# The shared chunk's product on GpSimd in place, and tables of finer steps of their own for the middle and last attention layers

## The chip, the cores and the metric

The kernel runs on one core of a Trainium2 chip. The metric is the device time of one execution in microseconds (us); the median of three runs is given. The core has TensorE (PE, matmul; its weight loads are PEld), VectorE (DVE), ScalarE (ACT), GpSimd (POOL) and SyncE (SP), each with an instruction queue of its own that runs in order. POOL and SP also issue the transfers (DMAs) of this kernel.

## The reference, cut to what matters

A graph network of four layers over N = 1024 nodes, B = 16 graphs and 128 features, all with the same adjacency matrix `adj`, in which about 8 of 1024 entries of a row are set. Layers L0, L2 and L3 are attention layers with 8 heads of 16 features, and L1 is a graph attention layer with one score per pair.

```python
# L0, L2, L3 (h is the layer's input)
Q, K, V = (h @ Wq, h @ Wk, h @ Wv)                 # heads of 16
scores = where(adj == 0, -inf, Q . K / sqrt(16))   # per head
x = h + (softmax(scores) @ V) @ Wo + bo
x = layer_norm(x, ln1_g, ln1_b)
x = layer_norm(x + relu(x @ W1 + b1) @ W2 + b2, ln2_g, ln2_b)
# L1
g = x @ W
e = leaky_relu(g @ a_src [i] + g @ a_dst [j]); e = where(adj == 0, -inf, e)
x = layer_norm(softmax(e) @ g + x, ln_gamma, ln_beta)
```

## The kernel before, in words

The kernel uses that the matrix is sparse. A setup sorts the nodes and makes lists of edges; the layers then fetch only the rows that edges name.

**Blocks.** The work is cut into 64 blocks, called units in the code: four layers, in each two halves of the graphs (GR = 2, eight graphs each), in each eight groups of 128 rows (T = 8). A row of a block has 8 graphs x 128 features = 1024 numbers (ROW).

**Parts and chunks.** The edges of a block are put into nine chunks. A chunk gives each of the 128 partitions one edge, and it is gathered as one transfer of 128 table rows, keys and values, from DRAM into a buffer `e` (L965, on POOL). Eight of the chunks belong to one group of 32 destination rows each. The ninth, the shared chunk (called MIX), takes the edges that are left over from two or three groups. An attention block has five parts: pairs of chunks are parts 0, 1, 2 and 4, and the shared chunk alone is part 3.

For each part of an attention block, DVE does three things in this order:

- `products`, L977: `pr` = keys of `e` times the queries. The queries of a pair lie in `qr`; those of the shared chunk in `qx`, which `shared` (L943) puts together by two to four SP copies from `qr`. There is one buffer `qx`, and four buffers `pr`.
- `exponentials`, L1000: sums of `pr` over the 16 features of a head; ACT then takes the exponential (`ex`, L1004).
- `weighted`, L1028: `pr` = values of `e` times `ex`, written over the products. It is done one part later.

PE then adds the rows of `pr` into `acc` with matrices of marks (`summed`, L1044), one to two parts later, and the exponentials likewise into the denominators. `divided` takes the reciprocal of the denominators (L1081) and makes `o` from `acc` (L1084), once per block, on DVE; POOL adds two small tiles into `seen` (L1097) for a check at the end.

**Gathers.** There are four buffers `e`, and gathers are issued up to four parts ahead: after the weighting of part i-1, POOL issues the gathers of part i+3 into the buffer that became free. `gathered` is called in this order by the main loop, one call per part.

**Tails.** What follows `o` in a block (output projection, normalisation, the two layers of the network behind it, second normalisation, and the next layer's keys and values) is `attention_tail` and `finish`. It runs in two halves, a and b, as generators of 18 steps each, during the next block. Steps of `attention_tail` are: transposes of `o` (PE, ACT copy), bias (ACT), Wo and `centre` (PE), normalisation in three steps (ACT), transposes, W1 in two steps (PE, ACT), W2 in two steps (PE), normalisation in three steps (ACT), transposes; then, in L0 and L2, two steps of the next layer's keys and values (`project`, PE and ACT, with SP stores to `kept`, L575, and `table`, L592 or L617), or, in L3, the transposes back into `outs` and the store of the output by POOL (L699).

**What sets the order.** Every engine runs its instructions in the order in which the program writes them; nothing is reordered. The main loop writes, for each part, the DVE work above, and between it calls `others()` three times. After an attention block, each of these 15 calls is an opening with a number, and a table gives the steps written there: `PLANS[layer][opening]` is a string in which `a` and `b` are one step of that half's tail and `q` is one step aside (the queries of the next block: Wq on PE, an ACT copy, four repeating matmuls on PE, four ACT copies into `qr`; then loads). Opening 0 comes at the end of part 1 of a block, right after the reciprocal and `o`; 1 to 3 lie in part 2, 4 to 6 in part 3, 7 to 9 in part 4, 10 to 12 in part 0 of the next block, and 13 and 14 in its part 1. Layer 1 has no table and spreads its steps evenly.

In part 1 the copies into `qx` are written after opening 13 and before opening 14, so on SP they stand ahead of every store of opening 14 and behind every store written before.

Of the kernel before, what the change touches and what calls it, by code (L numbers as in the profile page):

```python
# [18 lines left out]
ALU = mybir.AluOpType  # L19
# [29 lines left out]
ROW = G * D  # L49
# [17 lines left out]
MIX = J  # L67
# [51 lines left out]
def of_piece(v, piece):  # L119

    a, b = piece[0][0], piece[-1][0]
    if len(piece) == 2 and a == b:
        return v[:, a : a + 1].to_broadcast([v.shape[0], 2, v.shape[2]])
    return v[:, a : b + 1 : max(b - a, 1)]
# [21 lines left out]
def sparse_path(ctx: ExitStack, tc: tile.TileContext, a: dict, out: bass.AP, flag):  # L146


    nc = tc.nc
# [667 lines left out]
    def at_once(g):  # L817
# [12 lines left out]
        for t in range(T):  # L830
# [12 lines left out]

    PLANS = {
        0: (
            "qaaqqba", "baqba", "aq", "a", "bbaa", "abq", "baqbbaa", "", "aqbbba", "", "bbqaa", "b", "", "qqqqbbqq", "ba",
        ),
        2: (
            "qaaqqba", "baqba", "aq", "a", "bbaa", "abq", "baqbbaa", "", "aqbbba", "", "bbqaa", "b", "", "qqqqbbqq", "ba",
        ),  # L850
        3: (
            "qaaqqba", "baqba", "aq", "a", "bbaa", "abq", "baqbbaa", "", "aqbbba", "", "bbqaa", "b", "", "qqqqbbqq", "ba",
        ),
    }
    plan = [()]
# [6 lines left out]
    parts = []  # L862
# [7 lines left out]
    es, prs, exs, qs, qx, ofs, accums = {}, {}, {}, {}, {}, {}, {}  # L870

    def is_attention(u):
        return LAYERS[units[u][0]][1] is ATTN
# [76 lines left out]
    def gathered(i):  # L950
        if i >= len(parts):
            return
        u, pieces = parts[i]
        if u == T:
            while slow:
                while busy[0] and not held[0]:
                    advance(tails)
                advance(slow)
        l, g, t = units[u]
        width = tables[l, g].shape[1]  # L960
        many = 2 if is_attention(u) else J
        e = gather_buffer()
        es[i] = e[:, : many * width].rearrange("p (k c) -> p k c", k=many)
        for k, (j, r) in enumerate(sum(pieces, [])):
            nc.gpsimd.indirect_dma_start(  # L965
                out=es[i][:, k, :], out_offset=None, in_=tables[l, g][:, :],
                in_offset=bass.IndirectOffsetOnAxis(
                    ap=idx[:, min(l, 1), t, COLUMN[t, j, r] : COLUMN[t, j, r] + 1], axis=0
                ),
                bounds_check=N - 1, oob_is_err=False,  # L970
            )

    def products(i):
        u, (piece,) = parts[i]
        n = len(piece)
        prs[i] = [prods.tile([P, 2, ROW], F32, tag="pr", name="pr")]
        nc.vector.tensor_tensor(  # L977
            prs[i][0][:, :n, :], es[i][:, :n, :ROW],
            qx[u].rearrange("p (o c) -> p o c", o=1) if (MIX, 0) in piece
            else of_piece(qs[u], piece),  # L980
            ALU.mult,
        )

    def exs_of(i):

# [185 lines left out]
    with tc.manual_schedule():  # L1171
        wide = [gather_buffer() for _ in range(EDGES)]
        setup, entry, weights = graph(wide), at_once(0), load_weights("L0")
        next(setup)
        next(weights)
        next(entry)
        more = [weights, load_graph_weights()]
        rest = slots()
        first, second = loaded(0), loaded(1)
        for i, room in enumerate(setup):  # L1180
            if i == T:
                for gen in more:
                    next(gen)
            if room == "load":
                next(first)
            elif room == "spread":
                for _ in entry:
                    pass
                next(rest)
            elif room == "slots":  # L1190
                next(rest)
                for _ in first:
                    pass
                for _ in queries(0):
                    pass
                slow.append(at_leisure(1))
            elif room == "gather":
                for k in range(AHEAD - 1):
                    gathered(k)
                next(second)  # L1200
            else:
                for _ in range(room):
                    if next(entry, "end") == "end":
                        advance(slow)
                        break
        scratch.close()
        prods = ctx.enter_context(tc.tile_pool(name="prods", bufs=4))
        smalls = ctx.enter_context(tc.tile_pool(name="smalls", bufs=3))
        nc.gpsimd.memset(wide[3], 0.0)
        gathered(AHEAD - 1)  # L1210
        fronts.extend([islice(rest, WAIT + 2), second] + more)
        closing, sizes = None, ()
        begun = 0
        for i in range(len(parts) + 2):
            here = i < len(parts)
            u = parts[i][0] if here else len(units)
            if here:
                l = units[u][0]
                eager[0] = 1 if u < 2 else 0
                if i and parts[i - 1][0] != u:  # L1220
                    begun = i
                    if u < T - 1:
                        fronts.append(islice(rest, WAIT + 2))
                    if l + 1 < len(LAYERS) and LAYERS[l + 1][1] is ATTN:
                        if units[u][1:] == (0, 1):
                            more = load_weights(LAYERS[l + 1][0])
                            next(more)
                            next(more)
                        if units[u][1:] == (0, 4):
                            fronts.append(more)  # L1230
                if is_attention(u):
                    products(i)
            if i > 1:
                summed(i - 2)
                done = parts[i - 2][0]
                if parts[i - 1 : i] == [] or parts[i - 1][0] != done:
                    closing = divided(done)
                    next(closing)
            others()
            if here:  # L1240
                exponentials(i)
            if here and i == begun + 1:
                if is_attention(u):
                    shared(u)
                while loads:
                    advance(loads)
                if u + 1 < len(units):
                    fronts.append(queries(u + 1))
                loads.append(loaded(u + 2))
                if u:  # L1250
                    advance(loads)
            others()
            if 0 < i <= len(parts):
                weighted(i - 1, 0)
                if not is_attention(parts[i - 1][0]):
                    others()
                    weighted(i - 1, 2)
                gathered(i - 1 + AHEAD)
                for _ in sizes:
                    pass  # L1260
            if closing is not None and here:
                while any(gen not in free for gen in tails):
                    if opening[0] is None:
                        advance(tails)
                    else:
                        planned("ab")
                while opening[0] is not None and opening[0] < len(plan[0]):
                    planned()
                next(closing)
                sizes, closing = closing, None  # L1270
                passes = 3 if is_attention(u) else 4
                steps = STEPS if is_attention(done) else GRAPH_STEPS
                steps -= LATE[units[done][0]]
                pace[:] = 0.0, steps / (passes * sum(part[0] == u for part in parts) - 1)
                if is_attention(done) and opening[0] is None:
                    for gen in list(tails):
                        if gen in free:
                            for _ in gen:
                                pass
                            tails.remove(gen)  # L1280
                opening[0] = 0 if is_attention(done) else None
                plan[0] = PLANS.get(units[done][0], ())
            others()
            if i + 1 >= len(parts) or parts[i + 1][0] != u:

                while fronts:
                    advance(fronts)
        while opening[0] < len(plan[0]):
            planned()
        while tails:  # L1290
            advance(tails)
        for _ in closing:
            pass
        while tails:
            advance(tails)
# [435 lines left out]
```

## Time and profile before

| what | value |
|---|---|
| median of three runs | 2157.91 us (2153.96 to 2158.05) |
| the profiled execution's own time | 2143.22 us |
| its span, first to last instruction | 2141.5 us |
| mean granted TensorE clock | 0.97 |
| busy: PE, DVE, ACT, POOL | 91%, 86%, 71%, 49% of the span |
| mean DMA rate | 297 GB/s |
| DVE, shared chunk's products | 48 x 1.218 us |
| DVE, products of a pair | 192 x 2.30 us |
| POOL, gathers | 576 x 1.57 us, 8.1 us from issue to landing (median) |

Durations and waits come from the one profiled execution, which was about 15 us shorter than the median of the three runs. L0 takes the first third of the span (to about 707 us), L1 from there to about 1026 us, L2 to about 1580 us, and L3 the rest. Busy times of PE are modelled, since matmuls are pipelined. A wait row reads: who waited, for whom, how many us in all, how often, the longest.

### The profile page before, as it was taken

What the parts mean: (1) busy time and instruction counts of PE and PEld (TensorE: products, weight loads), DVE (VectorE), ACT (ScalarE), POOL (GpSimd) and SP (SyncE); (2) the same over time, 40 slices, a digit from 0 to 9 for tenths busy, and PEclk for the clock granted to TensorE, in tenths of its full rate; (3) what the DMA queues carried; (4) which work ended last, traced back from release to release, by engine and by line L of the source; (5) the groups of instructions that cost most, each with busy time, mean ns of one, the idle gap of its engine ahead of it and who ended that gap; (6) DMA issues with size and microseconds to landing.
All of it is one profiled execution on the core that took longest, in us unless ns stands there. A gap on an engine that the chain in (4) does not pass through costs nothing.

```text
span 2141.5 us, 37070 instructions
## 1 busy us (share of the span) xinstructions
PE 1954.5 (91%) x13444; PEld 1237.4 (58%) x13444; DVE 1852.2 (86%) x1368; ACT 1522.8 (71%) x5043; POOL 1048.6 (49%) x699
## 2 busy tenths in 40 slices
PE   6769999999999988997999999999998999898986
PEld 5545666666655555554566565666655555555554
DVE  6977999999997666677899999999998998989993
ACT  3437878878886554555687887778886878776874
POOL 3333445555456576784354544444443545545540
PEclk8789999999999999999999999999999999999998
DMA  7978888988988799998898998989988878687860
GB/s 272 348 271 291 309 300 313 312 287 316 318 314 288 271 324 323 347 376 309 295 338 310 334 312 293 321 324 319 320 303 297 288 277 297 233 311 260 313 227 22
DMA packets 164800, 636.10 MB, mean 297 GB/s; under 512 B 34664, under 2 KB 37480, under 8 KB 116110
## 3 DMA queue, kind: packets, MB, share of 16 engines
q0 software_dynamic: 88720, 485.08, 63.5%
q1 hardware_dynamic: 75888, 148.57, 20.5%
q8 instruction: 108, 1.77, 0.3%
q14 instruction: 84, 0.69, 0.1%
HBM read 581.08 MB, written 92.34 MB: 314 GB/s over the span
## 4 chain that ended last, share of the span: by engine, by line
PE 68%; DVE 11%; ACT 8%; issue 6%; DMA 4%; POOL 2%; POOLq 0%; DVEq 0%; ACTq 0%
PE acc L1044 17%; PE yps L752 7%; PE ps L654 7%; PE ps L738 7%; PE ps L583 6%; PE ps L929 6%; PE yps L728 4%; PE yps L727 4%; DMA e<-table,idx 4%; PE yps L756 3%; DVE pr L1028 3%; PE ps L920 2%; DVE pr L977 2%; DVE sc L1000 2%; ACT qr L932 2%
## 5 line engine op out<-in xcount | busy, mean ns | idle before, releaser
L965 POOL DMA_INDIRECT e<-table,idx x576 | 903.6, 1569 | 899.0 <-DVE pr L1028 708.8
L1028 DVE TENSOR_TENSOR pr<-e,ex 128x2048 f32<-128x2048 f32 (+1 forms) x320 | 662.2, 2077 | 56.8 <-ACT ex L1016 29.6
L1044 PE MATMUL acc<-pr,marks 128*32 128x512 f32 x2656 | 516.1, 605 | 36.3 <-DVE pr L1028 18.3
L977 DVE TENSOR_TENSOR pr<-e,qr 128x2048 f32<-128x2048 f32 x192 | 441.8, 2301 | 83.2 <-PE acc L1044 30.4
L1000 DVE TENSOR_REDUCE sc<-pr 128x128 f32<-128x2048 f32 (+1 forms) x240 | 497.4, 2073 | 8.1
L631 ACT ACTIVATE z<-yps,root 128x128 f32<-128x128 f32 x888 | 312.9, 368 | 70.4 <-PE yps L756 55.6
L1044 PEld LDWEIGHTS acc<-pr,marks 128*32 128x32 f32 x2656 | 109.7, 110 | 297.6 <-issue 246.9
L752 PE MATMUL yps<-W,f 128*128 128x128 f32 x1520 | 253.6, 285 | 16.9 <-ACT f L747 16.9
L752 PEld LDWEIGHTS yps<-W,f 128*128 128x128 f32 x1520 | 203.4, 191 | 99.3 <-ACT f L747 60.2
L647 ACT ACTIVATE z<-yps,rstd 128x128 f32<-128x128 f32 x888 | 251.0, 367 | 1.6
L587 ACT COPY kv<-ps 128x512 f32<-128x512 f32 x176 | 102.8, 588 | 175.3 <-PE ps L583 160.0
L932 ACT COPY qr<-ps 128x512 f32<-128x512 f32 x384 | 202.9, 602 | 22.2 <-PE ps L929 19.9
L583 PE MATMUL ps<-Wkv,xT 128*128 128x256 f32 x768 | 204.1, 409 | 12.7 <-ACT xT L660 5.5
L747 ACT ACTIVATE f<-ps,b 128x512 f32<-128x512 f32 x190 | 130.4, 687 | 87.9 <-PE ps L738 87.8
L738 PE MATMUL ps<-x,W 128*128 128x512 f32 x384 | 187.0, 610 | 1.3 <-ACT x L662 1.3
L631 ACT ACTIVATION_READ_ACCUMULATOR z<-yps,root 128x1 f32 x888 | 184.4, 208 | 0.0
L583 PEld LDWEIGHTS ps<-Wkv,xT 128*128 128x128 f32 x768 | 145.1, 201 | 67.5 <-issue 14.0
L654 PE MATMUL ps<-ident,z 128*128 128x128 f32 x896 | 148.9, 283 | 37.1 <-ACT qr L932 27.5
L654 PEld LDWEIGHTS ps<-ident,z 128*128 128x128 f32 x896 | 106.1, 142 | 89.0 <-ACT qr L932 62.3
L929 PE MATMUL ps<-q,rep 32*128 32x512 f32 x768 | 146.7, 663 | 8.6 <-ACT q L924 7.6
L727 PE MATMUL yps<-Wo,oT 128*128 128x128 f32 x768 | 153.2, 282 | 0.2
L728 PE MATMUL yps<-centre,x 128*128 128x128 f32 x768 | 152.6, 281 | 0.5 <-ACT x L723 0.2
(174 smaller groups left out, 2526.1 us busy)
## 6 DMA issues: line engine op xcount, KB each, us to landing
table<-kv SPq DMA_DIRECT2D x88, 512.0 KB, 7.5
kept<-xT SPq DMA_DIRECT2D x96, 256.0 KB, 5.1
x<-kept SPq DMA_DIRECT2D x48, 512.0 KB, 7.9
qx<-qr SPq DMA_DIRECT2D x54, 256.0 KB, 6.7
e<-table,idx POOLq DMA_INDIRECT x576, 8.1
table<-kv SPq DMA_DIRECT2D x32, 256.0 KB, 8.1
qx<-qr SPq DMA_DIRECT2D x48, 128.0 KB, 5.0
qx<-qr SPq DMA_DIRECT2D x12, 384.0 KB, 4.6
```

The costliest lines, as they stand in the source:

```text
L583: nc.tensor.matmul(ps[:, k, :], x[:, i + k, :], w[LAYERS[l][0], "Wkv"], start=True, stop=True,)
L631: nc.scalar.activation(z[:, i, :], y[:, i, :], AF.Square, scale=D**-0.5, bias=root, accum_out=total[:, i : i + 1],)
L647: nc.scalar.activation(z[:, i, :], y[:, i, :], AF.Copy, scale=rstd[:, i : i + 1])
L654: nc.tensor.transpose(ps[:, i, :], z[:, i, :], ident)
L738: nc.tensor.matmul(ps, p["W1"][:, f * P : (f + 1) * P], x1.rearrange("p g n -> p (g n)"), start=True, stop=True,)
L752: nc.tensor.matmul(ps[:, i, :], f1[:, f, i * P : (i + 1) * P], p["W2"][:, f, :], start=(f == 0), stop=False,)
L929: nc.tensor.matmul(ps, rep_of(j), q[32 * j : 32 * j + 32], start=True, stop=True)
L965: nc.gpsimd.indirect_dma_start(out=es[i][:, k, :], out_offset=None, in_=tables[l, g][:, :], in_offset=bass.IndirectOffsetOnAxis(ap=idx[:, ...
L977: nc.vector.tensor_tensor(prs[i][0][:, :n, :], es[i][:, :n, :ROW], qx[u].rearrange("p (o c) -> p o c", o=1) if (MIX, 0) in piece else of_p ...
L1000: nc.vector.tensor_reduce(sc[:, :n, :], prs[i][0][:, :n, :].rearrange("p k (a d) -> p k a d", d=HD), mybir.AxisListType.X, ALU.add,)
L1028: nc.vector.tensor_tensor(prs[i][k0 // 2][:, :m, :].rearrange("p k (a d) -> p k a d", d=d), es[i][:, k0 : k0 + m, base : base + ROW].rearr ...
L1044: nc.tensor.matmul(outs[32 * j : 32 * j + 32], marks[:, mark, :], rhss, start=(chunk == mine[0]), stop=(chunk == mine[-1]),)
```

## The change

Two parts. First, the product of the shared chunk is no longer made by DVE into a `pr` buffer but by GpSimd, over the queries in `qx` itself. It is written two parts ahead, behind the gathers of the part that is being written: for part 3 of a block that is at the end of part 1, behind the gathers of part 4. Its sum, its weighting (also in place, on DVE) and PE's sums then read `qx`, so `qx` stays in use until PE has summed the shared chunk. Second, L2 and L3 get tables of their own; the table of L0 stays as it was.

```diff
     PLANS = {
         0: (
-            "qaaqqba", "baqba", "aq", "a", "bbaa", "abq", "baqbbaa", "", "aqbbba", "", "bbqaa", "b", "", "qqqqbbqq", "ba",
+            "qaaqqba", "baqba", "aq", "a", "bbaa", "abq", "baqbbaa", "",
+            "aqbbba", "", "bbqaa", "b", "", "qqqqbbqq", "ba",
         ),
         2: (
-            "qaaqqba", "baqba", "aq", "a", "bbaa", "abq", "baqbbaa", "", "aqbbba", "", "bbqaa", "b", "", "qqqqbbqq", "ba",
+            "aabbqaaqaba", "", "qqa", "bb", "q", "", "b", "aaqba",
+            "", "aqaqbqqba", "qaqbqbbqb", "qb", "a", "", "baaabbb",
         ),
         3: (
-            "qaaqqba", "baqba", "aq", "a", "bbaa", "abq", "baqbbaa", "", "aqbbba", "", "bbqaa", "b", "", "qqqqbbqq", "ba",
+            "q", "qaabqaba", "", "qa", "aq", "qb", "ba", "qbbaqa",
+            "b", "aaqabb", "qb", "bqa", "ababb", "qqbq", "qaaabbb",
         ),
     }
...
     def products(i):
         u, (piece,) = parts[i]
+        if i in prs:
+            return
         n = len(piece)
         prs[i] = [prods.tile([P, 2, ROW], F32, tag="pr", name="pr")]
         nc.vector.tensor_tensor(
             prs[i][0][:, :n, :], es[i][:, :n, :ROW],
-            qx[u].rearrange("p (o c) -> p o c", o=1) if (MIX, 0) in piece
-            else of_piece(qs[u], piece),
+            of_piece(qs[u], piece),
             ALU.mult,
         )
+
+    def product_of_shared(i):
+
+        if i >= len(parts):
+            return
+        u, pieces = parts[i]
+        if not is_attention(u) or (MIX, 0) not in pieces[0]:
+            return
+        own = qx[u].rearrange("p (o c) -> p o c", o=1)
+        prs[i] = [own]
+        nc.gpsimd.tensor_tensor(own, es[i][:, :1, :ROW], own, ALU.mult)
...
                 gathered(i - 1 + AHEAD)
+                product_of_shared(i + 2)
                 for _ in sizes:
                     pass
```

## The prediction

> **What bounds the kernel now.** I read the busy rows of the page first, then stretches by layer, then the chain of waits by layer, then the waits of each engine, and last the order in time of one block. A block is one of the 64 units (layer, half of the graphs, 128 rows); its mark T0 is its reciprocal L1081.
>
> ```profile
> PE 1954.5 (91%) x13444; PEld 1237.4 (58%) x13444; DVE 1852.2 (86%) x1368; ACT 1522.8 (71%) x5043; POOL 1048.6 (49%) x699
> ```
> Three resources are nearly full. By stretches (PE, PEld, DVE, ACT, POOL busy; clock; DMA share; GB/s), steady parts of L0, L2, L3:
> ```profile
> 234.80:647.30 412.50, 395.80 (x2909) 256.00 (x2910) 392.31 (x237) 340.95 (x1180) 207.64 (x130) 1.00 0.88 308
> 1064.50:1580.30 515.80, 494.35 (x3345) 317.08 (x3346) 485.66 (x279) 414.31 (x1320) 240.37 (x149) 1.00 0.90 319
> 1616.40:2071.30 454.90, 417.50 (x2790) 255.12 (x2789) 421.11 (x235) 345.65 (x1120) 229.07 (x144) 0.97 0.80 283
> ```
> They hold 12, 15 and 13 blocks: 34.4, 34.4 and 35.0 us each. PE is 96%, 96% and 92% busy, DVE 95%, 94% and 93%. L3 projects no keys and values and still is no shorter: it waits.
>
> The chain of waits of 1064 to 1580 (L2) is PE with 3.2% on ACT qr L932, 2.0% on ACT f L747 and 1.7% on ACT kv L587, 6.9% or 2.4 us per block, and no DVE line among its thirteen. That of 1616 to 2037 (L3) has 11.5% on the landing of e and 14% on three DVE lines. So L2 hangs on PE's order, L3 on DVE and gathers too. One block of L2 (start, us, engine, line, tiles, idle before):
> ```profile
> 1512.84 0.55 DVE L1081 RECIPROCAL both<-ps 128x64 f32<-128x64 f32 x1
> 1513.42 1.29 DVE L1084 TENSOR_TENSOR o<-acc,both 128x512 f32<-128x512 f32 x2
> 1514.62 2.28 DVE L977 TENSOR_TENSOR pr<-e,qr 128x2048 f32<-128x2048 f32 x1
> 1516.94 2.29 DVE L1000 TENSOR_REDUCE sc<-pr 128x128 f32<-128x2048 f32 x1
> 1519.14 2.28 DVE L1028 TENSOR_TENSOR pr<-e,ex 128x2048 f32<-128x2048 f32 x1
> 1521.34 1.22 DVE L977 TENSOR_TENSOR pr<-e,qx 128x1024 f32<-128x1024 f32 x1
> 1522.59 1.22 DVE L1000 TENSOR_REDUCE sc<-pr 128x64 f32<-128x1024 f32 x1
> ...
> 1532.88 2.29 DVE L977 TENSOR_TENSOR pr<-e,qr 128x2048 f32<-128x2048 f32 x1 [0.85 <-DMA e<-table,idx]
> ```
> See the removed product at 1521.34 (T0+8.5), and 11.5 us later the next block's first product waiting for its gather. That gather is issued after the weighting of 1519.14 frees its buffer. So the removed instruction lies inside the gather's flight: removing it lets DVE arrive earlier at a wait.
>
> **What the Trainium skill says.** "SBUF — State Buffer", Who interferes with whom: a VectorE instruction with two SBUF inputs and a GpSimd instruction that reads SBUF block each other whole; the first holds the port, and tensor_reduce never contends. The trace agrees: the small GpSimd sum
> ```profile
> 1524.74 1.62 POOL L1097 TENSOR_TENSOR seen<-seen,both 128x128 f32<-128x128 f32 x1
> ```
> ends at 1526.36, 0.3 us after the L1028 product of 1523.73 to 1526.05, and its 128-element calls reach 2.5 us. Gather issues stretch likewise: 0.99 us alone, 2.94 at 1526.51 under a product. "GPSIMD Engine Reference", § 3.1, gives 4497 ns for a 2048-element f32 tensor_tensor; no run here shows one of this size. Estimate from it: half, 2.25 us.
>
> **Part 1: the shared chunk's product on GpSimd.**
> - Removed: 48 x 1.218 us = 58.4 us of DVE (the row pr<-e,qx), one per block. Also one of five uses of the four pr buffers per block (waits pr L977 <- PE acc: 30.4 us in all).
> - Added: 48 x 2.25 us on POOL. Below: 1.22, DVE's own time; above: 2.25 plus one blocked DVE product, 4.5. I take 2.25.
> - Its place: behind the fourth gather pair after T0. In the block above the two issues are at T0+0.35 and T0+1.64 (0.99 and 1.00 us), so it is asked for at T0+2.7. DVE's L977 holds the port until T0+4.1; then it runs beside the reduce to T0+6.35. The next two-input DVE operation is due at T0+6.3: a stall of 0 to 0.3 us. The cover is the reduce; without it, up to 2.25 us.
> - Behind it on POOL: the gather pair due at T0+8.9, 2.5 us later, and the seen sum. Waiting for it: the shared chunk's reduce, due at T0+8.6.
> - Its inputs: the qx copies were issued at T0-1.8 to T0 here, and a 256 KB one takes 6.7 us (its row). Now they must also wait for PE's sums of the previous shared chunk, since qx holds the product; between those sums and the denominators that L1081 waits for, PE has some 3.3 us of tail steps and 2.6 us of sums, so they end about T0-6 and the copies land near T0+1. No DMA is added; SP waits longer at the copies, with the x load and stores queued behind, which are due a block later.
> - The next gather: its first issue no longer meets the removed product (1.73 against 0.99 us, -0.7), its second meets the weighting, which now starts 1.2 us earlier (+1.0). DMA is 90% busy in L2, so I take the landing as 0.3 us earlier, between -0.7 and +1.0.
>
> **Part 2: the tables.** Each holds 18 a, 18 b and 15 q as before: nothing is added. What moves, with PE times from the timeline (four transposes 0.6, Wo and centre 1.8, W1 1.0 each, W2 half 1.35, Wkv half 0.92, Wq 0.95, four rep 1.1 to 1.4 us):
> - L2: reps (q) are no longer followed by a transpose that needs one of the four banks still being copied; Wo or sums stand between. This targets ps L654 <- ACT qr 12.5, yps L752 <- ACT f 5.5, ps L929 <- ACT q 3.3 us: 21.3 of PE's idle in L2. The kept and table stores move to opening 14, behind the qx copies on SP: the copies no longer wait behind the second kept store.
> - L3: opening 0 is only q, opening 1 begins with q: 2.4 us of PE work that needs no o, against ps L654 <- DVE o 20.5 us. But the final transposes of both halves move to opening 14, after exp and just ahead of the out store on POOL: one more PE and ACT step before it, about 1.2 us later.
>
> **The sum.** L0 keeps its table and its next gather lands 18.4 to 19.3 after T0 against a need at 19.1: 0.2 x 16 = -3 us. L2: 21.3 us of PE waits plus the 11.9 of pr waits are open, but its shortest block (33.3 us) and the gather limit it: 0.8 x 16 = -13. L3: -1.3 per block from o, DVE and pr, +1.0 from a late out store: -0.3 x 16 = -5. The end: more of the last-but-one block's tail stands after the last weighting, +2. Sum -19. The profiled execution took 2143.2 (span 2141.5), under the three runs shown, so it would be 2124; against the median of 2157.9 it is **2139 us** (-0.9%).
>
> **The rivals.**
> - A, slower: the GpSimd product comes late. In L3 the out store waits on POOL ahead of the gathers:
> ```profile
> 1617.76 1.02 POOL L699 DMA_INDIRECT out<-outs,places  x1 [8.87 <-ACT ex L1004]
> 1619.08 2.27 POOL L965 DMA_INDIRECT e<-table,idx  x1 [0.30 <-issue]
> 1621.66 0.99 POOL L965 DMA_INDIRECT e<-table,idx  x1 [0.31 <-issue]
> ```
> That block's T0 is 1616.38: the pair ends at T0+6.3, just when the weighting takes the port. The product then runs from T0+8.6 to 10.9: the reduce waits 2.3 for 1.2 saved, and the next gathers go 2.3 us later. It decides from a ready time of T0+4 on (free) to T0+6.3 (full price), and 8 of 14 blocks of L3 stand at the edge. Price 1.7 us per late block, midway between the 1.1 of the reduce and the 2.3 of the gathers: 16 of L3 and some 9 of L0 with late qx, +42; with L2's -13 and the end, up to 2190; half of them late, 2166. Against it: a longer block gives PE slack, so the out store moves earlier again.
> - B, no difference: the saving ends in the gather's flight, and the tables only exchange one ACT wait for another: 2154 to 2162.
> - C, full gain: L2 loses its 2.4 us of ACT waits and L3 falls to L2's busy PE: 48 x 1.2 = -58, 2100.
> - That the change is not made is no case: in the changed program's order POOL has 48 products and DVE none.
>
> **How the numbers follow.** My case 0.5, C 0.12, B 0.08, A 0.30. A measurement of this kernel tells 0.2% (4.3 us) from no change. Faster 0.61, same 0.08, slower 0.31. Range: from C's edge to the half of A that is likelier, 2102 to 2178; my case alone 2125 to 2150.
>
> **What would show it.** Right: a POOL row qx<-e,qx x48 of 2.2 to 4.5 us; DVE busy down by 58 us; ps L654 <- ACT qr nearly gone in L2 and <- DVE o in L3; L2 blocks of 33.5 us. Wrong: waits of DVE sc <- POOL qx over 30 us, gathers later than T0+8.9, POOL out waits grown, or blocks of L3 over 35.5 us.

## The result and the profile after

The changed kernel takes 2141.33 us (median of 7 runs, 2128.25 to 2147.82) against 2160.31 us (7 runs) of the kernel before beside it: ratio 0.9899, 95% interval [0.9869, 0.9929], so 1.0% faster. Its profiled execution has a span of 2126.4 us (before: 2141.5) at the same clock of 0.97.

Cut at the reciprocals (T0, now L1096), the two profiled executions differ so:

| us | setup | L0, 16 blocks | L1 | L2, 16 blocks | L3, 14 blocks | 15th block | rest |
|---|---|---|---|---|---|---|---|
| before | 150.0 | 556.9 | 319.4 | 553.9 | 491.0 | 30.3 | 39.9 |
| after | 147.7 | 562.1 | 320.1 | 536.9 | 487.2 | 32.0 | 40.3 |
| difference | -2.3 | +5.2 | +0.7 | -17.0 | -3.8 | +1.7 | +0.4 |

A segment of one and the same code differs by several us between profiles (L1, whose code only e11 below touches, lies between 312.8 and 320.1 over all kernels here), so of these only L2 stands out by itself: it carries the gain. From the page of the changed kernel, the busy row and two groups (line, engine, operation, tiles, count, busy us, mean ns, idle before and its releaser):

```profile
PE 1955.3 (92%) x13444; PEld 1240.3 (58%) x13444; DVE 1818.9 (86%) x1320; ACT 1516.5 (71%) x5043; POOL 1173.0 (55%) x747
L1043 DVE TENSOR_TENSOR pr<-e,ex 128x2048 f32<-128x2048 f32 x272 | 630.0, 2325 | 76.7 <-ACT ex L1019 38.4
L997 POOL TENSOR_TENSOR qx<-e,qx 128x1024 f32<-128x1024 f32 x48 | 134.4, 2800 | 62.3 <-DMA qx<-qr 34.5
```

DVE lost 48 instructions but 33 us only, not 58: its weightings (L1043) took 26.5 us more in all. The GpSimd product takes 2.80 us on average. The same stretches as before, of the changed kernel (span, then busy of PE, PEld, DVE, ACT, POOL, clock, DMA share, GB/s):

```profile
1065.00:1566.90 501.90, 495.07 (x3377) 319.94 (x3376) 475.13 (x265) 414.13 (x1334) 276.86 (x165) 1.00 0.96 329
1601.80:2054.10 452.30, 420.35 (x2807) 258.67 (x2806) 416.44 (x221) 342.66 (x1119) 270.03 (x156) 0.98 0.85 285
```

These are 15 blocks of L2 (33.5 us each; 34.4 before) and 13 of L3 (34.8; 35.0 before). In L2 PE went from 96% to 99% busy, and the transfers from 0.90 to 0.96. L3 changed little: PE from 92% to 93%, the transfers from 0.80 to 0.85. From the waits of the changed kernel, all engines (who, for whom, us in all, times, longest):

```profile
POOL out L699 <- ACT both L1109: 105.4, 13, 23.4
PEld ps L654 <- ACT qr L935: 43.2, 42, 1.5
POOL qx L997 <- DMA qx<-qr: 34.5, 13, 4.6
DVE sc L1015 <- POOL qx L997: 31.1, 11, 3.3
```

The second row was 107.1 us before: PE waits less for ACT, as the tables meant it to. In L3 PE's wait for `o` (20.5 us before) is gone too, but its wait for DVE's weighted products grew there from 1.1 to 25.1 us. The other three are the other side: the output's store (L699) waits 113 us on POOL in its two rows, against 99 in the three of before, the GpSimd product waits for the copies into `qx`, and DVE waits for the product. One such block of L3 (T0 = 1706.20), the timelines of DVE and POOL of the changed kernel:

```profile
1712.97 2.28 DVE L1043 TENSOR_TENSOR pr<-e,ex 128x2048 f32<-128x2048 f32 x1
1718.55 1.22 DVE L1015 TENSOR_REDUCE sc<-qx 128x64 f32<-128x1024 f32 x1 [3.30 <-POOL qx L997]
```
```profile
1708.62 3.01 POOL L699 DMA_INDIRECT out<-outs,places  x1 [5.99 <-ACT both L1109]
1711.94 1.01 POOL L968 DMA_INDIRECT e<-table,idx  x1 [0.30 <-issue]
1713.25 2.87 POOL L968 DMA_INDIRECT e<-table,idx  x1 [0.31 <-issue]
1716.15 2.37 POOL L997 TENSOR_TENSOR qx<-e,qx 128x1024 f32<-128x1024 f32 x1
1718.67 1.02 POOL L968 DMA_INDIRECT e<-table,idx  x1 [0.16 <-issue]
```

This is what rival A described: the store at T0+2.4, the gathers at T0+5.7, the product from T0+9.95 to 12.3, the reduce 3.3 us late and the next gathers at T0+12.5 (before: about T0+8.9).

### The profile page after: what moved, and what is told of

Its sections match the earlier page's. It is cut to its first block, busy times and chain, and to the rows that moved or that the text cites. A ratio compares the mean times of both kernels' runs of the same rounds, so it can differ in the third digit from the quotient of the medians.

```text
span 2126.4 us, 37294 instructions
## 1 busy us (share of the span) xinstructions
PE 1955.3 (92%) x13444; PEld 1240.3 (58%) x13444; DVE 1818.9 (86%) x1320; ACT 1516.5 (71%) x5043; POOL 1173.0 (55%) x747
## 4 chain that ended last, share of the span: by engine, by line
PE 47%; DVE 17%; DMA 14%; issue 13%; POOL 5%; ACT 4%; POOLq 0%; DVEq 0%; ACTq 0%
DMA e<-table,idx 13%; PE acc L1059 12%; DVE pr L1043 5%; PE yps L752 5%; PE ps L738 5%; PE ps L654 5%; DVE pr L982 4%; POOL e L968 4%; PE ps L583 3%; PE ps L932 3%; DVE sc L1015 3%; PE yps L756 2%; PE yps L728 2%; PE yps L727 2%; PE ps L923 2%
## 5 line engine op out<-in xcount | busy, mean ns | idle before, releaser
L968 POOL DMA_INDIRECT e<-table,idx x576 | 890.2, 1545 | 683.9 <-DVE pr L1043 417.9
L1043 DVE TENSOR_TENSOR pr<-e,ex 128x2048 f32<-128x2048 f32 x272 | 630.0, 2325 | 76.7 <-ACT ex L1019 38.4
L1059 PE MATMUL acc<-pr,marks 128*32 128x512 f32 x2200 | 442.8, 621 | 57.5 <-DVE pr L1043 43.9
L982 DVE TENSOR_TENSOR pr<-e,qr 128x2048 f32<-128x2048 f32 x192 | 440.4, 2294 | 43.1 <-ACT qr L935 21.0
L1015 DVE TENSOR_REDUCE sc<-pr 128x128 f32<-128x2048 f32 x192 | 438.9, 2286 | 6.6
L1059 PEld LDWEIGHTS acc<-pr,marks 128*32 128x32 f32 x2200 | 93.9, 111 | 292.6 <-issue 204.2
L583 PE MATMUL ps<-Wkv,xT 128*128 128x256 f32 x768 | 199.7, 406 | 15.2 <-ACT xT L662 7.4
L654 PE MATMUL ps<-ident,z 128*128 128x128 f32 x896 | 151.9, 286 | 20.9 <-ACT z L647 11.3
L997 POOL TENSOR_TENSOR qx<-e,qx 128x1024 f32<-128x1024 f32 x48 | 134.4, 2800 | 62.3 <-DMA qx<-qr 34.5
L932 PE MATMUL ps<-q,rep 32*128 32x512 f32 x768 | 141.3, 640 | 8.5 <-ACT q L927 7.7
```

Source lines behind the costliest of these rows:

```text
L583: nc.tensor.matmul(ps[:, k, :], x[:, i + k, :], w[LAYERS[l][0], "Wkv"], start=True, stop=True,)
L654: nc.tensor.transpose(ps[:, i, :], z[:, i, :], ident)
L932: nc.tensor.matmul(ps, rep_of(j), q[32 * j : 32 * j + 32], start=True, stop=True)
L968: nc.gpsimd.indirect_dma_start(out=es[i][:, k, :], out_offset=None, in_=tables[l, g][:, :], in_offset=bass.IndirectOffsetOnAxis(ap=idx[:, ...
L982: nc.vector.tensor_tensor(prs[i][0][:, :n, :], es[i][:, :n, :ROW], of_piece(qs[u], piece), ALU.mult,)
L1015: nc.vector.tensor_reduce(sc[:, :n, :], prs[i][0][:, :n, :].rearrange("p k (a d) -> p k a d", d=HD), mybir.AxisListType.X, ALU.add,)
```

## The experiments

Every ratio is to the kernel before, run in the same session; the segments come from the one profile of each kernel. "In place" means that the shared chunk's product is written over `qx`, as in the change.

| kernel | shared product | tables | ratio [95%] | L0 | L2 | L3 |
|---|---|---|---|---|---|---|
| before | DVE, `pr` | old | 1 | 556.9 | 553.9 | 491.0 |
| after | GpSimd, in place | new | 0.9899 [0.9869, 0.9929] | 562.1 | 536.9 | 487.2 |
| e1 | GpSimd, in place | old | 0.9921 [0.9893, 0.9949] | 561.6 | 556.2 | 475.3 |
| e2 | DVE, `pr` | new | 1.0100 [1.0075, 1.0124] | 555.8 | 567.1 | 508.0 |
| e3 | as after; L0: DVE, `pr` | new | 0.9902 [0.9881, 0.9923] | 556.3 | 540.9 | 485.3 |
| e4 | none | new | 0.9786 [0.9765, 0.9807] | 556.3 | 537.6 | 466.2 |
| e5 | as after, copies early | new | 0.9892 [0.9874, 0.9911] | 553.8 | 537.7 | 487.2 |
| e6 | as after, store behind | new | 0.9924 [0.9903, 0.9944] | 557.2 | 537.9 | 487.1 |
| e8 | as e3 | L2 new, L3 old | 0.9855 [0.9829, 0.9882] | 554.5 | 541.0 | 471.0 |
| e9 | DVE, in place | new | 0.9824 [0.9802, 0.9847] | 554.7 | 541.0 | 470.2 |
| e10 | DVE, in place | old | 0.9874 [0.9849, 0.9898] | 558.5 | 558.8 | 468.8 |
| e11 | DVE, own buffer | new | 1.0074 [1.0055, 1.0093] | 556.0 | 561.5 | 507.8 |
| e12 | L2 GpSimd, L0 and L3 DVE, in place | new | 0.9799 [0.9779, 0.9819] | 555.7 | 537.0 | 469.8 |
| e13 | DVE, `pr`, copies held | new | 0.9815 [0.9792, 0.9838] | 554.2 | 539.8 | 470.9 |

### One part at a time

**e1: the product alone** (the changed kernel with the old strings in `PLANS[2]` and `PLANS[3]`).

> Part 1 alone: the product on GpSimd, with the table of before in all three attention layers. Theory T1 (the tables make the gain, the product alone is neutral or worse because it waits for late qx copies and late out stores): ratio to before 0.998 to 1.008; blocks of L2 34.4 us or longer, DVE waiting for POOL qx over 30 us in all. Rival T2 (the 58 us taken off DVE make the gain): ratio 0.988 to 0.993, blocks of L2 near 33.3 us.

**e2: the tables alone** (the kernel before with the new strings).

> Part 2 alone: the new tables of L2 and L3, the product on DVE as before. T1: L2 loses its waits of PE for ACT, 0.5 to 0.8 us per block, L3 stays within 5 us: ratio 0.992 to 0.997. T2: the tables only rearrange: 0.998 to 1.004. A third reading, that only both together gain: alone each is 1.000 and the gain is in neither.

The product alone is faster (0.9921), by L3 alone: 491 to 475 us. In L2 it does nothing. The tables alone are **slower**, 1.0100: L2 +13 and L3 +17 us. Yet together they take 17 us off L2. So neither part's gain is what the prediction had it as, and the tables need something that the product brings.

**e3: L0's shared product back on DVE, in a `pr` buffer.**

```diff
         nc.vector.tensor_tensor(
             prs[i][0][:, :n, :], es[i][:, :n, :ROW],
-            of_piece(qs[u], piece),
+            qx[u].rearrange("p (o c) -> p o c", o=1) if (MIX, 0) in piece
+            else of_piece(qs[u], piece),
             ALU.mult,
         )
...
-        if not is_attention(u) or (MIX, 0) not in pieces[0]:
+        if not is_attention(u) or (MIX, 0) not in pieces[0] or units[u][0] == 0:
             return
```

> The changed kernel, but in L0 the product stays on DVE in a pr buffer. T1: L0 gives back the 5 us that it lost against before (from the end of setup to the end of L0), so 4 to 7 us under the changed kernel, ratio to before 0.986 to 0.989. T2: DVE's relief helps in L0 too, so this is 3 us or more over the changed kernel, ratio 0.991 or more.

**e4: no product.** The kernel leaves the shared chunk's product out, so its output is another one.

```diff
         prs[i] = [own]
-        nc.gpsimd.tensor_tensor(own, es[i][:, :1, :ROW], own, ALU.mult)
```

> The changed kernel with the shared chunk's product left out altogether: its scores are the sums of the queries alone, so the output differs. DVE is relieved, and POOL has neither the work, nor the wait, nor the port. If the removed DVE product lies in the gather's flight in all blocks, this is within 5 us of the changed kernel (ratio 0.988 to 0.991). If the late and port-holding POOL product is what costs, up to the 31 us that DVE waited for it come back: 12 to 30 us under the changed kernel, ratio 0.976 to 0.985, most of it in L3 and L0.

Both bring L0 to 556 us, so L0's loss goes with GpSimd's product. Its size isn't firm: e1 and e6 have the L0 code of the change and take 561.6 and 557.2 us, and with the product on DVE L0 lies between 554.2 and 558.5. A ratio does not tell these few us either (e3: 0.9902). Without the product L2 is as long as with it (537.6 against 536.9), so there it is hidden whole; L3 falls by 21 us, so there it is not.

### L3: the store, the table

**e6: the output's store behind the gathers and the product on POOL** (the store of a block is put into a list and issued behind `product_of_shared`).

> The changed kernel with the output store of L3 written on POOL behind the gathers and the shared product of the same part, not ahead of them. The product alone had L3 at 475 us (from the 49th to the 63rd reciprocal), both parts 487, no product at all 466. If the late store is what holds the gathers and the product back under the new L3 table, L3 falls to 466 to 476 us, ratio to before 0.980 to 0.986. If the table itself orders PE badly in L3, L3 stays at 483 or more.

The product is on time then, and L3 does not move: 487.1 us. From the waits of DVE in L3 (e6, 1563.1 to 2050.2), and POOL's timeline of a block with T0 = 1701.63:

```profile
DVE pr L983 <- DMA e<-table,idx: 26.0, 8, 4.6
```
```profile
1701.98 0.99 POOL L969 DMA_INDIRECT e<-table,idx  x1 [3.93 <-DVE pr L1044]
1703.27 0.99 POOL L969 DMA_INDIRECT e<-table,idx  x1 [0.30 <-DMA e<-table,idx]
1704.97 3.03 POOL L998 TENSOR_TENSOR qx<-e,qx 128x1024 f32<-128x1024 f32 x1 [0.70 <-PE ps L654]
1708.15 3.06 POOL L700 DMA_INDIRECT out<-outs,places  x1 [0.16 <-issue]
1711.52 2.98 POOL L969 DMA_INDIRECT e<-table,idx  x1 [0.30 <-DVE sc L1016]
1714.81 1.88 POOL L969 DMA_INDIRECT e<-table,idx  x1 [0.31 <-issue]
```

No wait for POOL's product is left, but the next pair of gathers, whose buffer is free from T0+8.6, is issued at T0+9.9 and 13.2, and the second of them lands at T0+21.2, 0.1 us before DVE begins the next block's first product after a wait of 3.6 us (the trace puts the end of that wait to a step of PE). The store, the pair, the product and the next pair must all pass POOL within some 9 us; whichever is last is the one waited for. That is read from this block, not tested by itself.

**e8: e3 with the old table in L3.**

> The best choice of each layer so far: L0 with the product on DVE and its old table, L2 with the product on GpSimd and the new table, L3 with the product on GpSimd and the old table. If the layers add up as measured one by one (L0 556, L2 537, L3 475 us), the profiled execution is about 2105 to 2112 us and the ratio to before 0.980 to 0.985. If the gains depend on the layer before, it is no better than the changed kernel, 0.988 or more.

L3 falls to 471.0 us with the product on GpSimd: under the old table the store is issued earlier (T0-0.2 to +1.4 in e8, T0+0.1 to +4.2 in the change), and POOL has room for the product.

### On DVE, in place

**e9: new tables, the product on DVE at its old place, over `qx`; e10: the same with the old tables.**

```diff
     def products(i):
         u, (piece,) = parts[i]
-        if i in prs:
+        n = len(piece)
+        if (MIX, 0) in piece:
+            own = qx[u].rearrange("p (o c) -> p o c", o=1)
+            prs[i] = [own]
+            nc.vector.tensor_tensor(own, es[i][:, :1, :ROW], own, ALU.mult)
             return
-        n = len(piece)
...
-                product_of_shared(i + 2)
```

> New tables; the shared product stays on DVE, at its old place in DVE's order, but is made in place over the queries, so it no longer takes one of the four pr buffers. Tables alone had L2 at 567 and L3 at 508 us, both parts 537 and 487. Theory D (DVE's 1.2 us per block and the earlier gather matter): L2 560 to 568, ratio 1.006 to 1.012. Theory R (five products in four buffers tie DVE to PE's sums, and the freed buffer is what lets the new table work): L2 536 to 545, ratio 0.990 to 0.998.

> Tables of before, the shared product on DVE but in place over the queries, so only the pr buffer is freed. Product on GpSimd alone had L3 at 475 us against 491 before, and L2 unchanged at 556. Theory D: no gain, L3 488 to 494, ratio 0.998 to 1.003. Theory R: L3 falls to 474 to 480, ratio 0.992 to 0.995.

e9 is faster than the change, 0.9824, with all 48 products still on DVE. So GpSimd is not the gain but a price: L0 +7 and L3 +17 us between e9 and the change, L2 -4. Only L3's is clear of the spread between profiles: the L2 code of the change takes 536.9 to 541.0 us in the five kernels that have it (the change, e3, e5, e6, e8), and e9's L2 takes 541.0. What gains goes with writing over `qx`. At this point I took the freed `pr` buffer for the reason: four uses per block of four buffers instead of five.

### Why in place gains: the buffer, or the copies

**e11: out of place, into a buffer of its own.** `pr` is freed here too, but `qx` is not held. (The edit is shown against e9; a pool for the new buffer is added, and to make room a small buffer of L1 has two copies, not three.)

```diff
-            prs[i] = [own]
-            nc.vector.tensor_tensor(own, es[i][:, :1, :ROW], own, ALU.mult)
+            prs[i] = [alone.tile([P, 1, ROW], F32, tag="px", name="px")]
+            nc.vector.tensor_tensor(prs[i][0], es[i][:, :1, :ROW], own, ALU.mult)
```

> New tables; VectorE makes the shared chunk's product at its old place, out of place, into a 4 KB buffer of its own that nothing else uses; the pr buffers stay four, and now serve four products a block in place of five. (To make room, the small buffer 'of' of the graph layer has two copies, not three.) Theory 'the freed pr buffer is the gain': like the product in place on VectorE, L2 about 541 us, L3 about 470 us, ratio to the kernel before 0.980 to 0.986. Rival 'being in place is the gain' (one read stream fewer, or the qx buffer released later): no better than the new tables alone, L2 about 567, L3 about 508, ratio about 1.01.

1.0074: the freed buffer is **not** the gain. e11 and e9 differ in which buffer the product goes to, and so in when `qx` is free. Out of place, it is free once the product has read it; in place, once PE has summed the shared chunk, some 14 us later. SP's copies into it for the next block, and the load of `x` (512 KB) behind them, go when it is free. From the DVE waits of L3, first e9 (1566.8 to 2037.0), then e11 (1585.9 to 2093.7):

```profile
DVE pr L985 <- DMA e<-table,idx: 10.5, 11, 3.2
```
```profile
DVE pr L985 <- DMA e<-table,idx: 51.6, 20, 5.4
```

**e13: only the time of the copies, and of the load behind them.** Nothing in place, nothing on GpSimd, five `pr` uses as before; e2 with one small read of `qx`, two parts later:

```diff
             if here:
                 exponentials(i)
+            if 1 < i < len(parts) and is_attention(parts[i - 2][0]) and (MIX, 0) in parts[i - 2][1][0]:
+                last = smalls.tile([P, 1], F32, tag="last", name="last", bufs=1)
+                nc.vector.tensor_copy(last, qx[parts[i - 2][0]][:, :1])
```

> The kernel before with the new tables, nothing in place, the shared product on VectorE in one of the four pr buffers as before; one small read of qx (128x1, VectorE) is added two parts after the shared product, behind that part's sum of scores, so that SP's copies into qx for the next block can go no earlier than about 9 us ahead of its T0 (with the tables alone they went 19 to 23 us ahead of it in L2 and L3). Theory 'in place gains because it holds qx until TensorE has read it, and so keeps the copies out of the way of the gathers': L2 falls from 567 to 541 to 547 us, L3 from 508 to 470 to 474 us, DVE's waits of pr for landed gathers go, ratio to the kernel before 0.981 to 0.987. Rival 'the freed pr buffer is needed as well': part of it only, L2 over 553, L3 over 485, ratio over 0.99. Rival 'the copies' time is a by-product': no better than the tables alone, ratio about 1.01.

0.9815, L2 539.8 and L3 470.9: the whole gain of e9, from 47 reads of 0.14 us. (The intervals of e13 and e9 overlap.) SP's timeline in one block of L3, first e2 (its T0 1700.0, the next 1737.1), then e13 (1669.0, the next 1701.6):

```profile
1709.87 1.18 SPq L945 DMA_DIRECT2D qx<-qr  x2
1712.64 0.33 SPq L897 DMA_DIRECT2D x<-kept  x1
```
```profile
1692.86 1.30 SPq L945 DMA_DIRECT2D qx<-qr  x2
1694.20 0.84 SPq L897 DMA_DIRECT2D x<-kept  x1
```

In e2 they go at T0+9.9, in e13 at T0+23.9. DVE's timelines of these blocks, e2 and e13:

```profile
1718.69 1.22 DVE L1030 TENSOR_TENSOR pr<-e,ex 128x1024 f32<-128x1024 f32 x1
1723.64 2.29 DVE L979 TENSOR_TENSOR pr<-e,qr 128x2048 f32<-128x2048 f32 x1 [3.73 <-DMA e<-table,idx]
```
```profile
1687.00 1.22 DVE L1030 TENSOR_TENSOR pr<-e,ex 128x1024 f32<-128x1024 f32 x1
1688.13 2.28 DVE L979 TENSOR_TENSOR pr<-e,qr 128x2048 f32<-128x2048 f32 x1
1690.45 2.29 DVE L1002 TENSOR_REDUCE sc<-pr 128x128 f32<-128x2048 f32 x1
1692.65 0.14 DVE L1246 COPY last<-qx 128x1 f32<-128x1 f32 x1
```

The product at T0+19.1 is the one that the prediction showed waiting; its gathers are issued at T0+8.9 and 11.0 in both kernels. In e2 the copies follow at T0+9.9, so both are in flight together, and the gather is late by 3.7 us. The gathers of 14 blocks of L3 (count, median us from issue to landing), e2, then e13:

```profile
e<-table,idx POOLq DMA_INDIRECT x126, 10.5
```
```profile
e<-table,idx POOLq DMA_INDIRECT x126, 7.8
```

Set side by side, when the first copy is issued against the T0 that comes before the product using it, in us and without the first two blocks of a layer, and what the layer takes:

| kernel | L2 copies | L2, us | L3 copies | L3, us | DVE waits for landed gathers, L2, L3 |
|---|---|---|---|---|---|
| e2 | -19 to -24 | 567.1 | -23 to -29 | 508.0 | 22.7, 43.4 |
| e11 | -19 to -23 | 561.5 | -23 to -29 | 507.8 | 22.3, 51.6 |
| before | -1 to -3 | 553.9 | -21 to -27 | 491.0 | 9.2, 17.0 |
| e10 | -1 to -4 | 558.8 | -5 to -6 | 468.8 | 16.0, 3.3 |
| e9 | -8 to -12 | 541.0 | -8 to -11 | 470.2 | 3.4, 10.5 |
| e13 | -9 to -10 | 539.8 | -9 to -12 | 470.9 | 2.2, 9.2 |

In L3, held copies make 469 to 471 us with either table. With early ones it is 491 under the old table and 508 under the new, though the first copies go at much the same time; but under the old table the load of `x` behind the copies goes some 17 us ahead of the next T0 (median), and in e2 some 24. There the gathers land after 8.4 us, against 10.5 in e2 and 7.8 in e13. That points to the load and the last copy more than to the first copy; but every edit here that holds the copies holds the load behind them too, so which of them delays the gathers is not shown. Nor is the freed `pr` buffer ruled out under the old table: there the copies were held only in place (e1, e8, e10), which frees it as well, and before the change DVE waits 9.2 us of L3 for such a buffer.

In L2 the old table keeps the copies back anyway, behind the second kept store; the new table puts the stores behind the copies, sets these free to go at once, and so costs 13 us until something holds them. Held, the new table gains 13 to 17. How much of that is PE's waits gone and how much the copies at T0-8 in place of T0-2 stays open: no run had the old table with copies at T0-8 in L2.

The Trainium skill ("DMA: Bandwidth & Descriptors", SWDGE vs HWDGE vs iDMA) says that transfers issued by GpSimd and by the hardware generators (as SP's are) feed different queues of a DMA engine, which takes turns between them. The longer landing (10.5 against 7.8 us) agrees with it; no run here shows the turns themselves.

### L0, and the three layers put together

**e5: the copies of a block written one part earlier** (`shared(u)` at `i == begun`).

> The changed kernel with the qx copies of a block issued one part earlier. Theory 'L0 loses because qr's copies into qx come late, behind a block's second kept store on SP, and the GpSimd product waits for them': the product of the first block of L0 parts is on time, L0 falls from 562 to about 556 us, L2 and L3 stay at 537 and 487, ratio to the kernel before 0.985 to 0.989. Rival 'L0 loses because GpSimd's product stretches VectorE's work there by the shared port': L0 stays at 561 to 563, ratio 0.989 to 0.993. Side: SP's copies now wait where the stores stood, and could hold back kept stores; then L0 is longer than 563.

L0 is 553.8 us and its copies go at T0-4.3 to -6.4 (T0-1.0 to -3.4 in the change). DVE's waits in L0 for GpSimd's product go with it: 9.0 us in the change and in e1 (L0 562.1 and 561.6), 2.2 in e6 (557.2), none in e5. So the late copies are the likely cause of L0's loss, as far as a few us in single profiles can tell; the ratio (0.9892) doesn't tell e5 from the change's 0.9899.

**e12: GpSimd in L2 alone.**

```diff
-        if not is_attention(u) or (MIX, 0) not in pieces[0]:
+        if not is_attention(u) or (MIX, 0) not in pieces[0] or units[u][0] != 2:
             return
```

with `products` as in e9 for L0 and L3.

> The changed kernel with the shared chunk's product on VectorE, in place, in L0 and L3; on GpSimd, in place, in L2 alone. If the three layers add up as the runs so far have them one by one (L0 555, L2 537, L3 470): 3 to 5 us under VectorE in place throughout, ratio to the kernel before 0.979 to 0.984. If moving the product in L2 buys nothing that the profile can show: equal to VectorE in place throughout, 0.982.

The layers add up as expected (555.7, 537.0, 469.8). At 0.9799 it is the fastest kernel here that makes all 48 products, but its interval overlaps those of e9 and e13: what GpSimd gives in L2, at most 4 us, isn't shown by the times.

## Why the prediction was right, and where it was not

The sum was -19 us, measured -15.1 between the profiles, and -19.0 between the medians; the time and the side were right. That the time came out so close is luck in part: the terms of L2 and L3 were right in size for other reasons than those given, and three of the four signs named for "wrong" came true (waits of DVE sc for POOL qx of 31.1 us, gathers later than T0+8.9, longer POOL waits at the output's store); the fourth, blocks of L3 over 35.5 us, did not (34.8 on average). The terms:

- **L2, -13; measured -17.** The size stands: blocks of 33.5 us as named, and of PE's waits in L2 for `qr` at L654 and for `f` (18.0 us) 0.7 us is left. (The same L2 code gave -13 in e3 and e8.) The credit was wrong: Part 2 gave it to the tables, which alone cost 13 us here (e2). They pay only with the copies, and the load behind them, held.
- **L3, -5; measured -3.8.** Right as a number, wrong as a sum: it was "-1.3 per block from o, DVE and pr, +1.0 from a late out store". It is -20 from the new table with held copies (e13; -21 in e9) and +17 from GpSimd (e9 against the change); that the two come to about -5 is luck. The +17 is rival A's mechanism. A's price was 1.7 us for each of 16 late blocks, 27 us, or half of that if half of them are late; in the trace 6 of the 14 blocks wait, 2.3 to 3.3 us each.
- **L0, -3; measured +5.2.** The failed step is "the copies land near T0+1", drawn from a block of L2 and used for all. In L0, where the old table stays, the copies still go at T0-1.0 to -3.4, the product starts at T0+2.5 to 7.0, and the reduce waits. Rival A had named this too ("some 9 of L0 with late qx"): 9 blocks at 1.7 us, 15 us or half of it, which is more than was measured. The +5.2 is itself no firm size (e6: +0.3 with the same L0 code).
- **The end, +2; measured +2.1.** This is no proof: the last segment alone lies between 39.2 and 43.1 us over the kernels here.
- **Part 1's removed product, taken as hidden in the gather's flight.** Right in L2: with and without any product it is 537 to 541 us (e4, after, e9).
- **Part 1's `pr` buffer.** Freed alone, under the new tables, it gave 6 us in L2, little more than the spread between profiles, and nothing in L3 (e2 against e11). The step that carries the change was in the text, "now they must also wait for PE's sums", and was weighed only as a delay of the product. That the copies and the load behind them had been running under the critical gather was not seen; with them held DVE's waits for landed gathers in L3 are 9.2 us (e13), against 17.0 before.
- **GpSimd's product, 2.25 us (1.22 to 4.5).** 2.35 to 2.39 where no two-input DVE instruction is ahead of it, 2.80 on average, 4.51 at most. The stall of DVE, "0 to 0.3 us" a block, is 0.55: 26.5 us in longer weightings. Hence DVE busy fell by 33 us, not 58.
- **Rivals.** B is out. C's 2100 would be a ratio of 0.973; e12 comes nearest (0.9799), and with the products back on DVE in two layers. A's late product is there in L3 and in some blocks of L0, and is paid for by the held copies and L2. (Half of A's late blocks come to 2168 by A's own terms, not the 2166 written; nothing rests on it.)

## What to carry to other kernels

A buffer's release can set when the next transfer into it starts, and an early start is no gain where that transfer runs beside one that is waited for: look at what each queue issues within the flight of the critical transfer, and at what lets it go. In place, or one small late read, is a cheap way to hold such a transfer back. Before work is moved to an idle engine, count what its queue must pass within the window between two of its critical issues, not its busy share.

## What the runs showed of the hardware

- A two-input DVE instruction and GpSimd's product hold each other up whole, and either may come first. DVE's weighting row in the changed kernel (min, median, max ns), and GpSimd's product:

```profile
L1043 DVE TENSOR_TENSOR pr<-e,ex x272: 1216/2282/4499, 101.8 to 2075.1; 128x2048 f32<-128x2048 f32 x128, 128x1024 f32<-128x1024 f32 x8
```
```profile
L997 POOL TENSOR_TENSOR qx<-e,qx x48: 2354/2380/4508, 110.1 to 2063.7; 128x1024 f32<-128x1024 f32 x48
```

  A weighting that starts 0.03 us behind the product takes 4.49 us, which is 2.28 and most of the product's 2.36; the product of 4.51 us starts within 0.01 us of a weighting that takes its plain 2.28. The Trainium skill ("SBUF — State Buffer", Who interferes with whom) says that the ports which the two share are an exclusive lock, and that the order of issue decides who blocks; both orders are seen here. The maximum of the weighting was 2.60 us before.
- An issue of the output's store on POOL took 1.02 us alone, and as long when a two-input DVE instruction started after it. It took 3.01 to 3.07 us when that instruction had started 0.14 to 0.18 us before it (the change and e6). The gathers' issues stretch too (0.99 alone, up to 3.1).
- Copies and a load issued beside the gathers raised the gathers' median time to landing in L3 from 7.8 to 10.5 us, with 8.4 us in the kernel before, where the last copy and the load go later than in e2.
